# Dealing the raw groups' normalizations and products into the first three groups of a graph layer's loop

## The chip, the core and the metric

The kernel runs on one core of a Trainium2 chip. A core has five engines with a queue each: PE (TensorE, matmuls; its weight loads are listed as PEld), DVE (VectorE), ACT (ScalarE), POOL (GpSimd) and SP (SyncE, which here only issues DMAs). The metric is the device time of one execution in microseconds. The profile shows one execution of it, with every instruction's start and length; "clock" is the share of full TensorE speed that the throttle granted.

## The reference

`x` holds 12500 nodes of 128 values; 200000 edges lead from `src` to `dst`, sorted by `dst`, each of one of four types.

```python
h = jnp.maximum(_layernorm(x, axis=-1), 0.0)
xs = h[src]
for i in range(4):
    mask = (edge_type_4 == i)[:, None]
    msgs = msgs + jnp.where(mask, xs @ W[i] + b[i], 0.0)
out = x + segment_sum(msgs, dst, num_segments=N)
```

Edges are worked on in chunks of 128. The draw of `dst` puts many edges on the first nodes and few on the last.

## The kernel before, in words

**Three kinds of chunks.** The first `C0` = 528 chunks go to about 1480 much-used nodes. They are not gathered: for each of these nodes the kernel counts how often each source node and type occurs (a *slot* is one chunk's share of a node) and multiplies the counts with the whole table of normalized rows. The chunks behind them are taken in groups of `G` = 16. Groups 0 to 2 (`RAW` = 3) are the *raw* groups: their rows of `x` are gathered before the table exists, and are normalized by themselves. Groups 3 and up are the loop's: their rows are gathered from the finished table `htab`.

**The prologue.** It normalizes all nodes and writes `htab` in bfloat16 triples (`first_part` to `third_part`), gathers the raw rows (`gather_raw`, tile `hx`), and builds the slots (`make_slots`). Here the framework's scheduler sets the order on every engine. Then `add_up_raw` runs for the raw groups, one after the other: statistics and one-hots on DVE (`looks`, `oh`), 16 normalizations on ACT (L461), products of rows with one-hots on PE in float32 (L635), counts by type (L641), the weight product (L648) into the bank `raw_py`, and copies by ACT between them. All 48 columns sets are copied once to an `xo` buffer (L1283).

**The loop** (from `ordered` on) keeps the program's own order on PE, DVE and ACT. Each group has eight parts of two chunks. In a part PE multiplies the pair's rows with their one-hots (L578); a stretch of `dense_work`, the counting, follows; then DVE gets its share of the side work: one-hots of the next group (L561), adds of the group before into the ring of sums (`ring_adds`, L666), flushes of finished stretches of the ring (L691 to L713), which are decided by `goes`. The group before is weighed in the first and third part (L596, L603, L605). DVE makes a slot's two one-hots (L957 and L965, or L961), PE counts a unit of two or three slots with L983, ACT copies it (L989). The slots' one-hots are made in sets of four, about two sets ahead of PE. Units are counted in batches: 20 units first, then 27 each. When a batch is counted, `multiply` streams the table through four buffers `hs` (L1029, 576 KB each, issued by SP) and multiplies (L1033, three a node block), beside the counting of the next batch. `pace` says how far the counting must be after each part: equal numbers of PE columns for each group from `LEAD` = 3 to the last full one, where a group's own columns count too.

**Queues.** POOL issues the loop's gathers (L544), one DMA a chunk, 16 a group, one group ahead, into 11 buffers for two chunks each. The gathers of the first groups are held by `gates`: before, nine normalizations of the raw rows (`ties`) and ten marks of slot-making. SP issues the table's writes, the `hs` loads, the next blocks' indices (L210) and the loads and stores of results.

Of the kernel before, what the change touches and what calls it, by code (L numbers as in the profile page):

```python
# [35 lines left out]
F32 = mybir.dt.float32  # L36
# [31 lines left out]
LEAD = RAW  # L68
SOON = (RAW * 16) + HG
# [5 lines left out]
def kernel(  # L75
# [171 lines left out]
    rawp = early.enter_context(tc.tile_pool(name="raws", bufs=RAW * G // HG))  # L247
# [139 lines left out]
    iota_f = prep.tile([P, KR], F32, name="iota_f", bufs=1)  # L387
    nc.vector.tensor_copy(iota_f, iota_i[:, :KR])
# [29 lines left out]
    pick_f = prep.tile([P, NT, N3], F32, name="pick_f", bufs=1)  # L418
    nc.vector.tensor_copy(pick_f, pick)

# [11 lines left out]
    def look(xt, n, tag, wide):  # L432

        sums2 = aheads.tile([P, wide, 2], F32, name="mv" + tag)
        var = aheads.tile([P, wide], F32, name="var" + tag)
        rstd = aheads.tile([P, wide], F32, name="rstd" + tag)
        nmr = aheads.tile([P, wide], F32, name="nmr" + tag)
        st = aheads.tile([P, wide, 2, 3], F32, name="st" + tag)
# [171 lines left out]
    def add_up_raw(t0, g, rows, marked):  # L610
        win = window_of(C0 + t0)
        K = NT * win
        row = lambda k: rows(k)
        looks, spread, root, scales, normalize = look(row, g, "r", G)
# [4 lines left out]
        oh = rawp.tile([P, G, KR], F32, name="ohf", bufs=2)[:, :, :K]  # L619
# [8 lines left out]
        done = [normalize(k, row(k)) for k in range(g)]  # L628
        marked.extend(done[4::5])
        yield True  # L630
        sb = spool.tile([P, G * KM], F32, name="sb")[:, : G * K].rearrange("p (g t n) -> p g t n", g=G, t=NT)
        for i0 in range(0, g, SG):
            ps = s_ps.tile([P, 512], F32, name="ps")[:, : SG * K].rearrange("p (i n) -> p i n", i=SG)
            for i in range(i0, i0 + SG):
                nc.tensor.matmul(ps[:, i - i0, :], rows(i), oh[:, i, :], start=True, stop=True)  # L635
# [3 lines left out]
        pc = s_ps.tile([P, 512], F32, name="ps")[:N3, : G * win].rearrange("p (g n) -> p g n", g=G)  # L639
        for t in range(NT):  # L640
            nc.tensor.matmul(pc, pick_f[:, t, :], ohv[:, :, t, :], start=(t == 0), stop=(t == NT - 1))  # L641
        cnt = spool.tile([N3, G * WIN], BF16, name="cnt")[:, : G * win].rearrange("p (g n) -> p g n", g=G)
# [623 lines left out]
    for g in groups:  # L1266
        for _ in g:
            pass
# [35 lines left out]
    for gi, (t0, g) in list(enumerate(zip(starts, sizes)))[RAW:]:  # L1304
# [17 lines left out]
        for j, part in enumerate(sum_up(t0, g, *now, gi >= FULL)):  # L1322
# [5 lines left out]
            for f in late:  # L1328
                f()
# [192 lines left out]
```

## Time and profile before

| | |
|---|---|
| runs | 1647.18 us median of 3 (1646.1 to 1649.81) |
| profiled execution | 1651.06 us, span 1649.2 us |
| busy share of the span | PE 88%, DVE 63%, POOL 61%, ACT 28% |
| mean granted clock | 0.957 |
| moved by DMA | 317.02 MB, 192 GB/s |

Groups of instructions are named by line, engine, operation and tiles. A row of the busy time by stage gives the stretch, its length, then for each engine busy microseconds with the number of instructions, then the clock, the share of DMA time and the DMA rate. Rows of the timeline and of the chain of waits begin with start and length in microseconds. Matmuls overlap, so the starts of neighbouring rows tell the rate of PE, and their lengths do not.

### The profile page before, as it was taken

The numbers are of one execution on the slowest core, as the hardware profiler recorded it, in microseconds if no ns is written. First come the engines' busy times: TensorE is split into PE (matmuls) and PEld (weight loads), VectorE is DVE, ScalarE is ACT, GpSimd is POOL, SyncE is SP. The second block draws the span as 40 slices with busy tenths as digits, with TensorE's granted clock in tenths as the row PEclk, the third lists the DMA queues.
The fourth block names the chain that finished last, engine by engine and source line by source line (L and its number), as shares of the span: only waits on it lengthen the run. The fifth ranks groups of instructions, "written<-read, shape, count | busy, mean of one in ns | idle before, by whom it ended". The sixth has DMA issues, their size and how long they took to land.

```text
span 1649.2 us, 33169 instructions
## 1 busy us (share of the span) xinstructions
PE 1457.4 (88%) x11293; PEld 958.5 (58%) x11293; DVE 1041.5 (63%) x5387; ACT 458.7 (28%) x1121; POOL 1011.6 (61%) x1062
## 2 busy tenths in 40 slices
PE   5678789999899999999999999999999999998975
PEld 2236476666566566666666666656565656565654
DVE  8792977666585766657576666657564756574333
ACT  6494222222222222222222222222222222222011
POOL 7435566666666666666666666666666566666562
PEclk9785799999999999999999999999999999999997
DMA  7452377766667766666666667666666566666652
GB/s 221 129 212 75 107 220 220 217 197 213 200 206 211 217 194 212 197 208 208 207 202 201 200 209 220 181 210 203 180 219 198 175 194 211 184 189 193 210 169 70
DMA packets 138411, 317.02 MB, mean 192 GB/s; under 512 B 25880, under 2 KB 78666, under 8 KB 138235
## 3 DMA queue, kind: packets, MB, share of 16 engines
q1 hardware_dynamic: 89323, 214.61, 41.7%
q0 software_dynamic: 48912, 100.24, 20.8%
q8 instruction: 89, 1.46, 0.4%
q14 instruction: 87, 0.71, 0.1%
HBM read 298.71 MB, written 16.04 MB: 191 GB/s over the span
## 4 chain that ended last, share of the span: by engine, by line
PE 81%; issue 8%; DVE 8%; ACT 2%; DMA 1%; DVEq 0%; SPq 0%; POOL 0%; ACTq 0%
PE pa L1033 47%; PE pt L983 12%; PE py L605 7%; PE ps L578 7%; DVE o L957 1%; PE pt L1047 1%; PE ps L635 1%; PE py L596 1%; PE pt L691 1%; DVE oh L561 1%; DVE o L965 1%; DVE ring L666 1%; PE pt L857 1%; DVE stt L440 1%; PE pt L854 0%
## 5 line engine op out<-in xcount | busy, mean ns | idle before, releaser
L544 POOL DMA_INDIRECT hm<-htab,srcT x987 | 954.7, 967 | 575.6 <-issue 226.0
L1033 PE MATMUL pa<-counts,hs 128*128 128x324 fp8e4 (+1 forms) x5586 | 1000.5, 304 | 50.2 <-issue 47.1
L1033 PEld LDWEIGHTS <-hs 128*128 128x128 bf16 x5586 | 519.0, 96 | 325.1 <-issue 84.7
L957 DVE TENSOR_SCALAR o<-iota_n,hkT 128x392 bf16<-128x392 f16 x1211 | 401.2, 331 | 75.4 <-PE pt L983 30.6
L983 PE MATMUL pt<-o,o 128*128 128x396 bf16 x1211 | 378.4, 336 | 37.0 <-DVE o L965 20.0
L989 ACT CAST counts<-pt 128x396 int32<-128x396 f32 x506 | 242.1, 493 | 500.5 <-PE pt L983 172.1
L561 DVE TENSOR_SCALAR oh<-iota_b,keyT 128x56 bf16<-128x56 bf16 (+8 forms) x987 | 167.7, 261 | 265.6 <-PE ps L578 94.6
L581 ACT COPY sb<-ps 128x224 f32<-128x224 f32 (+8 forms) x247 | 98.4, 399 | 480.3 <-PE pt L983 165.0
L578 PE MATMUL ps<-oh,hm 128*128 128x56 bf16 (+8 forms) x2961 | 189.1, 198 | 38.0 <-issue 35.3
L578 PEld LDWEIGHTS <-hm 128*128 128x128 bf16 x2961 | 163.0, 99 | 96.5 <-issue 49.1
L666 DVE TENSOR_TENSOR ring<-ring,py 128x14 f32 (+7 forms) x960 | 167.7, 175 | 65.0 <-PE pa L1033 13.0
L965 DVE TENSOR_SCALAR o<-iota,loT 128x128 bf16<-128x128 bf16 x660 | 178.4, 270 | 0.0
L983 PEld LDWEIGHTS <-o 128*128 128x128 bf16 x1211 | 114.8, 97 | 96.2 <-DVE o L965 27.4
L965 DVE TENSOR_SCALAR o<-iota,loT,byT 128x128 bf16<-128x128 bf16 x461 | 155.4, 337 | 0.0
L605 PE MATMUL py<-sb,wsb 128*128 128x224 f32 (+7 forms) x480 | 129.5, 412 | 1.3 <-issue 1.0
L605 PEld LDWEIGHTS py<-sb,wsb 128*128 128x128 f32 x480 | 88.2, 196 | 27.6 <-issue 5.6
L997 DVE COPY bi<-counts 128x27 int32<-128x27 int32 (+1 forms) x19 | 4.2, 220 | 113.3 <-issue 64.7
L528 POOL DMA_INDIRECT hx<-in_x_dram,srcT x48 | 51.3, 1069 | 35.9 <-DVE stt L440 22.4
L600 ACT CAST cnt<-py 128x224 bf16<-128x224 f32 (+7 forms) x60 | 23.7, 396 | 93.3 <-PE ps L578 29.9
L461 ACT ACTIVATE h<-hm,nmrt,rstdt 128x128 f32<-128x128 f32 x98 | 43.0, 493 | 1.0 <-DVE mvt L444 0.5
L1047 PE MATMUL pt<-sd,wsb 128*128 128x81 f32 (+1 forms) x152 | 25.8, 325 | 4.6 <-issue 4.6
L490 PE MATMUL ps<-h,ident 128*128 128x384 f32 (+1 forms) x34 | 16.3, 563 | 12.7 <-issue 11.6
(235 smaller groups left out, 666.6 us busy)
## 6 DMA issues: line engine op xcount, KB each, us to landing
hs<-htab SPq DMA_DIRECT2D x304, 576.0 KB
hm<-htab,srcT POOLq DMA_INDIRECT x987
htab<-h SPq DMA_DIRECT2D x32, 288.0 KB
xo<-in_x_dram SPq DMA_DIRECT2D x24, 256.0 KB
out_dram<-xo SPq DMA_DIRECT2D x24, 256.0 KB
hs<-htab SPq DMA_DIRECT2D x19, 192.0 KB
hm<-in_x_dram SPq DMA_DIRECT2D x18, 192.0 KB
hm<-in_x_dram SPq DMA_DIRECT2D x14, 168.0 KB
```

The lines of the kernel that those rows point to most:

```text
L528: one = nc.gpsimd.indirect_dma_start(out=hm[:, i * D : (i + 1) * D], out_offset=None, in_=x, in_offset=bass.IndirectOffsetOnAxis(ap=srcf[: ...
L544: one = nc.gpsimd.indirect_dma_start(out=hm[:, (i - h0) * D3 : (i - h0 + 1) * D3], out_offset=None, in_=htab, in_offset=bass.IndirectOffse ...
L561: nc.vector.tensor_scalar(oh[:, i, :], iota_b[:, :K], keyf[:, at : at + 1], None, ALU.is_equal)
L578: nc.tensor.matmul(ps[:, i - i0, :], rows(i, c), oh[:, i, :], start=(c == 0), stop=(c == 2))
L581: nc.scalar.copy(sb[:, i0:i1].rearrange("p g t n -> p g (t n)"), ps[:, : i1 - i0, :])
L605: nc.tensor.matmul(py[:, :g, :], wsb[:, t, :], sb[:, :g, t, :], start=False, stop=(t == NT - 1))
L666: nc.vector.tensor_tensor(to, to, of(i), ALU.add)
L957: one = nc.vector.tensor_scalar(o2[:, k, :NB], iota_n, hkT[:, s : s + 1], None, ALU.is_equal)
L965: one = nc.vector.tensor_scalar(o1[:, k], iota_1, loT[:, s : s + 1], by, ALU.is_equal, ALU.mult)
L983: one = nc.tensor.matmul(pb, o1, o2, start=first, stop=last)
L989: nc.scalar.copy(counts[:, :, i * NT : (i + 1) * NT], pb.rearrange("p (b t) -> p b t", t=NT))
L1033: nc.tensor.matmul(pa[:, : 3 * nu * NT].rearrange("p (m v) -> p m v", m=3), hs[:, j - j0, c * D : (c + 1) * D], of, start=(j == 0 and c == 0),
```

## The change

The raw groups' products and most of their normalizations are dealt into the loop. Before the loop only the statistics, the one-hots and the scales of the three groups and the first four normalizations of group 0 are left. `raw_work` goes through 18 steps (six for each raw group: four of four products each with the next four normalizations, one of type counts, one of the weight product), spread over the 24 parts of loop groups 3, 4 and 5. The products take their PSUM banks from `x_ps` (four, shared with the counting) instead of `s_ps`, and have their own `sbr` and `cntr` tiles.

`pace` adds `RAW_COLUMNS` = 1920 columns for each chunk to each of these three groups, so that less counting falls into them and more into each later group. The pool of raw rows stays open until the end of group 5, on the right side of memory; therefore the second buffer of counts (`dense2`) and the four `hs` buffers come only then. The copy of the raw sums follows group 5, all 48 raw ring adds are dealt in group 6, and the earliest group with a flush is 4 instead of 3. The gates of the first gathers are 19 marks of slot-making.

```diff
+RAW_COLUMNS = 1920
...
-    rawp = early.enter_context(tc.tile_pool(name="raws", bufs=RAW * G // HG))
...
+        for k in range(SG):
+            normalize(k, rows(k))
+        yield True
+        sb = rawp.tile([P, G * KR], F32, name="sbr", bufs=1)[:, : G * K].rearrange("p (g t n) -> p g t n", g=G, t=NT)
         for i0 in range(0, g, SG):
-            ps = s_ps.tile([P, 512], F32, name="ps")[:, : SG * K].rearrange("p (i n) -> p i n", i=SG)
+            ps = x_ps.tile([P, 512], F32, name="pt")[:, : SG * K].rearrange("p (i n) -> p i n", i=SG)
             for i in range(i0, i0 + SG):
                 nc.tensor.matmul(ps[:, i - i0, :], rows(i), oh[:, i, :], start=True, stop=True)
+            for k in range(i0 + SG, min(i0 + 2 * SG, g)):
+                normalize(k, rows(k))
             nc.scalar.copy(sb[:, i0 : i0 + SG].rearrange("p g t n -> p g (t n)"), ps)
             yield True
...
-        next((i for i in [*range(RAW, FULL), final - 1] if starts[i] + sizes[i] >= c), final)
+        next((i for i in [*range(RAW + 1, FULL), final - 1] if starts[i] + sizes[i] >= c), final)
...
-        own = [columns(i) for i in range(LEAD, last)]
+        own = [columns(i) + (G * RAW_COLUMNS if i < LEAD + RAW else 0) for i in range(LEAD, last)]
...
-                now = vs, dense.tile([P, NW + 1, UB * NT], I32, name="counts")
+                now = vs, dense[batches.index(vs) % 2].tile([P, NW + 1, UB * NT], I32, name="counts")
...
     for g in groups:
-        for _ in g:
-            pass
+        next(g)
+        next(g)
+    next(groups[0])
+
+    def raw_work():
+        for m, g in enumerate(groups):
+            for n, _ in enumerate(g):
+                if n == G // SG - 1 and m + 1 < RAW:
+                    next(groups[m + 1])
+                yield True
...
-    gates.extend(ties + marks[len(marks) - (20 - 1 - len(ties)) :])
+    gates.extend(marks[-19:])
+    raw_steps = raw_work()
+    raw_done = 0
+    raw_all = RAW * (G // SG + 2)
...
+        if gi == 2 * RAW:
+            side += raw_adds
...
+            while gi < 2 * RAW and raw_done < raw_all and raw_done * RAW * parts < ((gi - RAW) * parts + j + 1) * raw_all:
+                next(raw_steps)
+                raw_done += 1
...
+        if gi == 2 * RAW - 1:
...
+            nc.scalar.copy(raw_sums, raw_py[:, : RAW * G * win_raw])
...
+            raw_stack.close()
+            dense.append(counting.enter_context(tc.tile_pool(name="dense2", bufs=1)))
+            hsp = counting.enter_context(tc.tile_pool(name="hsp", bufs=STREAM))
```

More of the change, by code (lines that the diff above doesn't have):

```diff
@@ L607, in weigh, with add_up_raw @@
         yield True
[L610 removed]
+    def add_up_raw(t0, g, rows):
         win = window_of(C0 + t0)
         K = NT * win
[L613 to L614 removed]
+        looks, spread, root, scales, normalize = look(rows, g, "r", G, rawp, RAW)
         for l in looks:
```

55 lines of the change are left out of this document (25 added, 30 removed).

## The prediction

> **What bounds the kernel now.** I read the page's busy shares and slices first, then the busy time by stage, the chain of waits around 118 to 154 us, the timelines of POOL and DVE there, and the first L596 matmul of each group as the border between groups (the row of 232.40 below is group 5's, issued behind the first pair of group 6).
>
> ```profile
> span 1649.2 us, 33169 instructions
> PE 1457.4 (88%) x11293; PEld 958.5 (58%) x11293; DVE 1041.5 (63%) x5387; ACT 458.7 (28%) x1121; POOL 1011.6 (61%) x1062
> ...
> PE   5678789999899999999999999999999999998975
> ...
> PEclk9785799999999999999999999999999999999997
> ...
> L1033 PE MATMUL pa<-counts,hs 128*128 128x324 fp8e4 (+1 forms) x5586 | 1000.5, 304 | 50.2 <-issue 47.1
> ...
> L666 DVE TENSOR_TENSOR ring<-ring,py 128x14 f32 (+7 forms) x960 | 167.7, 175 | 65.0 <-PE pa L1033 13.0
> ```
> ```profile
> 232.40 0.26 PE L596 MATMUL py<-oh,three 128*32 128x192 bf16 x3
> ```
> ```profile
> core 0: us, PE busy (x) PEld busy (x) DVE busy (x) ACT busy (x) POOL busy (x), PEclk, DMA share, GB/s
> 117.34:154.18 36.84, 33.17 (x141) 28.42 (x142) 10.26 (x55) 22.32 (x63) 21.01 (x22) 0.50 0.37 120
> 154.18:180.50 26.32, 13.10 (x98) 6.01 (x98) 20.84 (x107) 8.77 (x22) 17.15 (x18) 0.69 0.32 87
> 180.50:206.36 25.86, 22.31 (x186) 16.00 (x185) 24.22 (x136) 7.29 (x19) 13.74 (x15) 0.77 0.44 128
> 206.36:232.40 26.04, 23.27 (x218) 18.61 (x217) 21.41 (x93) 7.34 (x18) 16.79 (x16) 0.93 0.73 229
> 232.40:257.23 24.83, 22.67 (x213) 17.26 (x212) 17.08 (x94) 5.47 (x14) 15.27 (x16) 1.00 0.70 221
> 257.23:279.98 22.75, 21.30 (x184) 14.40 (x183) 16.05 (x82) 6.01 (x16) 14.52 (x16) 1.00 0.70 215
> 232.40:1596.88 1364.48, 1255.82 (x10139) 832.91 (x10139) 843.17 (x4443) 325.53 (x778) 866.59 (x897) 0.99 0.66 202
> ```
>
> The first row is the raw stage: groups 0 to 2 alone, PE busy 33 of 37 us at half clock. The next three are loop groups 3, 4 and 5, paced by DVE (24.22 of 25.86 us busy in group 4), which makes the one-hots of slots. From 232.40 on PE sets the pace: 92% busy at a clock of 0.99, 57 groups in 1364.48 us, 23.9 us each.
>
> So two things can be saved, the 37 us in which nothing but raw work runs and the slack of three DVE-paced groups, and there is one place where they are paid back: each matmul that leaves groups 3 to 5 comes again in the PE-bound part.
>
> **The change part by part.** *What is moved.* The instruction order of both programs gives the work between the L596 borders. Before, groups 3, 4 and 5 hold 97 slot-counting matmuls (L983, 128x396) and 216 multiplying ones (L1033, 128x240). Changed, they hold 31 and none, and beside them the raw work: 48 rows, 12 pick matmuls and 12 of L648's kind. Thus 66 and 216 matmuls are deferred. Group 6 then holds 36 and 72 (before 23 and 99), group 7 28 and 135 (before 23 and 102). The 48 raw ring adds move from groups 3 and 4 into group 6.
>
> *When the loop can reach group 6.* The gathers of the loop's rows are issued one by one on POOL:
>
> ```profile
> 117.34 0.94 POOL L544 DMA_INDIRECT hm<-htab,srcT  x1 [21.56 <-ACT rstdr L452]
> 118.59 0.95 POOL L544 DMA_INDIRECT hm<-htab,srcT  x1 [0.30 <-issue]
> ...
> 127.56 0.95 POOL L544 DMA_INDIRECT hm<-htab,srcT  x1 [0.30 <-issue]
> 132.14 0.94 POOL L544 DMA_INDIRECT hm<-htab,srcT  x1 [3.64 <-ACT hx L461]
> ```
> ```profile
> 279.37 0.94 POOL hm L544
> ...
> 280.62 2.97 DMA hm<-htab,srcT
> ```
>
> They start when the table is written, at 117.34, and step by 1.25 us. Before, they were held by normalizations (3.64 us at 132.14), harmlessly, for PE was busy with raw work. The changed gates are marks of slot-making, which is over when the table ends, so only the table holds the first gather. On SP the first index load of the next block now stands among the last table writes, for +0.3 us, and the four loads of hs no longer follow them:
>
> ```profile
> 115.72 1.90 SPq L1029 DMA_DIRECT2D hs<-htab  x4
> 154.18 0.33 SPq L210 DMA_DIRECT2D si<-in_src_dram  x1
> ```
>
> A group needs 16 gathers, 20 us. The second gather of group 6 is number 50: 117.6 + 49 x 1.25 = 178.9; a gather lands 4.2 us after its start (279.37 to 283.59), so 183.1. With that pair's matmuls and counting, the border that stood at 232.40 comes at 184.5 if nothing is slower than POOL.
>
> Is anything slower? PE, at the raw stage's half clock:
>
> ```profile
> 135.19 4.97 PE ps L635 x24
> 140.17 2.24 PE ps L641 x8
> ...
> 144.08 2.43 PE pa L648 x8
> ```
> ```profile
> 188.66 2.21 PE py L605 x8
> 190.88 0.20 PE ps L578 x6
> ...
> 193.37 0.64 PE pa L1033 x6
> 194.00 0.17 PE pt L983
> ...
> 273.23 0.43 PE pa L1033 x3
> ```
>
> Raw: 96 halves x 0.207 = 19.9 us, picks 3 x 2.24, products 3 x (2.43 + 0.24). Own: 144 of L578 at 0.04 = 5.8, two L605 sets 5.3. Counting 31 at 0.34 (twice the full-clock 0.17) = 10.5. Sum 56 us against 60 us of gathers; PE can start at about 124, when DVE has made the first set, which ends at 180 without a wait. So PE is just under POOL. DVE has some 10 to 13 us a group to do, ACT 16 normalizations a group (6.27 us by the row below) plus copies, some 12 us. I take 184.5; below, 182.5 (a landing of 2.2 us); above, 26 us a group, as these groups took before, 202.
>
> ```profile
> 117.50 6.27 ACT L461 ACTIVATE hx<-hx,nmrr,rstdr 128x128 f32<-128x128 f32 x16 [0.35 <-DVE nmrr L456]
> ```
>
> *Group 6.* DVE now has the ring adds of all three raw groups:
>
> ```profile
> 163.91 0.78 DVE L666 TENSOR_TENSOR ring<-ring,xo 128x10 f32 x4 [1.15 <-issue]
> 164.62 0.32 DVE L957 TENSOR_SCALAR o<-iota_n,hkT 128x392 bf16<-128x392 f16 x1
> ...
> 168.22 0.77 DVE L666 TENSOR_TENSOR ring<-ring,xo 128x10 f32 x4
> ...
> 210.03 1.60 DVE L561 TENSOR_SCALAR oh<-iota_b,keyT 128x48 bf16<-128x48 bf16 x9
> ...
> 214.95 1.75 DVE L708 TENSOR_TENSOR acc<-acc,ring 128x1536 f32<-128x1536 f32 x1
> 217.09 1.34 DVE L713 MEMSET ring<- 128x1536 f32 x1 [0.39 <-DVE acc L708]
> ```
>
> By the order, PE's last counting of group 6 needs 34 slots (eight took 164.62 to 168.22: 0.45 each, 15.3), 48 raw adds (four in 0.71: 8.6), 13 row one-hots (0.17: 2.2), three register loads (by L666's row 65.0 us idle over 960/16 = 60 sets: 1.1 each, 3.3), sums 0.8 and the copy of the raw sums 0.8. That is 31 us against 24.83 before: +6.2 (bounds 24.8, as before, and 36, with each load at twice its price and the slots at 0.5). PE's own work there is 18 us at full clock, so DVE decides; if PE fell to half clock there, 31 too. Behind the adds on DVE stand the slots that PE waits for, and SP's next load into a sums buffer (xo) with the fifth load of hs behind it; the four first hs loads cover exactly the 72 multiplications of group 6, so this costs nothing unless the adds last past the group. Those four loads (formerly prefetched at 115.72) now wait for the last raw product and have some 10 us of counting to land behind.
>
> *Group 7* has the first flush (1.75 + 1.34), now a group later, and 28 slots, 24 adds, 19 one-hots, two loads: 26 us of DVE, 26.5 taken, against 22.75: +3.7.
>
> *The deferred matmuls.* At the end of group 7 the changed kernel is behind by 48 slots (143 less 95) x 0.167 = 8.0 us, 87 narrow multiplications x 0.107 = 9.3 and 123 wide ones x 0.143 = 17.6: 34.9 us of PE at full clock, dealt over 55 groups. The loop's PE is 92% busy, and what idles there is mostly issue; I take 37, between 26 (a quarter fills idle time) and 38 (34.9 / 0.92).
>
> *The sum against the profiled span:* 184.5 - 232.4 = -47.9; +6.2; +3.7; +37: -1.0 us, 1648 us of span. The profiled execution took 1651.06 (span 1649.2 and 1.9 around it), 3.9 above the median 1647.18 of the runs shown; the same difference gives 1646. Copies of iota_f and pick_f, pool places and the PSUM buffers of x_ps instead of s_ps I cost at nothing: the two copies (each no larger than a ring add's kind) replace two that the program made before, and the PSUM buffers are freed by ACT copies, from a queue with some 12 us of work in 20; without that cover each of groups 3 to 5 would lose the 1 to 2 us that are in the slower rival.
>
> [...] The clock during the raw stage:
>
> ```profile
> 132.00:136.00 4.00, 4.00 (x18) 3.78 (x17) 0.00 (x0) 4.00 (x11) 2.94 (x4) 0.50 0.18 49
> 148.00:152.00 4.00, 4.00 (x20) 3.88 (x20) 0.00 (x0) 0.58 (x2) 3.08 (x4) 0.50 0.31 85
> ```
>
> PE was busy all of both stretches and still had half clock: the short float32 products do not raise it here, so I count groups 3 to 5 at half clock. [...]
>
> **The rivals.** *PE, not POOL, paces groups 3 to 5 (slower).* The 56 us of half-clock work fill 93% of the gather time, in a fixed order in which each raw product waits for ACT, each slot for DVE and each pair for its gather. If waits add 3 us a group, 23 us a group, the border comes at about 193: +8.5, so 1655. Groups 5 and 6 before took 26.04 and 24.83 although no engine was busy beyond 23.27, which speaks for it; against it, that each raw step has a step's time between its parts. It decides against the change from 21.5 us a group on (border 188.8). Chance 0.36.
>
> *The deferred matmuls are cheaper (faster).* PE idles 108.7 us between 232.40 and 1596.88. If a quarter of the deferred matmuls falls into stretches in which PE would have waited for DVE or a gather, 37 becomes 26, -11: 1636. For it, that 108.7 us are there; against it, that at L1033 47.1 of 50.2 idle us are issue, which comes with each instruction wherever it stands. A clock that rises in group 6 doesn't help, DVE bounds it. Chance 0.26.
>
> *Paid back as summed (no change).* Chance 0.38. That the counting isn't thinned is excluded by the order: 31 against 97.
>
> **How the numbers follow.** A measurement of this kernel can tell about 0.2%, 3.3 us. The likeliest single case is no change, 1646, its own range 1643 to 1650. The range takes in the faster rival short of its end (1638: border at 182.5, deferred at 30) and the slower one past its price (1658: border at 196). Faster 0.26, same 0.38, slower 0.36.
>
> **What would show it.** After: gathers 1.25 us apart from 117.5 to about 178 with hardly a wait for PE; the border of group 6 at 183 to 187; PE clock about 0.5 to 0.7 till then; group 6 near 31 us with DVE full; group 7 near 26; later groups 0.6 to 0.7 us longer than before. The prediction is wrong if gathers wait for PE before 178, if group 6 takes 24 or 36 us, or if later groups grow by less than 0.4 us or more than 0.9.

## The result, and the profile after

The changed kernel took 1658.88 us (median of 4 runs, 1655.3 to 1660.82) beside 1646.64 us of the kernel before (1646.04 to 1649.81): a ratio of 1.0061, 95% interval [1.0045, 1.0077], slower by 0.6%. Forecast were 1646 us and no change.

Busy time by stage of the changed kernel (the columns are those of the first row). The stages are: up to the first gather of the loop, groups 3, 4 and 5 up to the border of group 6 (the L591 matmul, L596 before), group 6, group 7, the later groups, the end.

```profile
core 0: us, PE busy (x) PEld busy (x) DVE busy (x) ACT busy (x) POOL busy (x), PEclk, DMA share, GB/s
0.00:118.84 118.84, 78.14 (x288) 32.74 (x288) 99.93 (x448) 80.38 (x205) 54.36 (x76) 0.91 0.55 175
118.84:169.30 50.46, 19.11 (x122) 15.18 (x122) 17.27 (x86) 11.51 (x32) 34.66 (x36) 0.51 0.27 71
169.30:192.83 23.53, 16.61 (x121) 13.92 (x120) 8.57 (x48) 10.64 (x32) 15.17 (x16) 0.71 0.26 71
192.83:215.27 22.44, 18.12 (x115) 12.96 (x114) 10.18 (x56) 9.23 (x27) 14.73 (x16) 0.64 0.28 69
215.27:252.62 37.35, 21.47 (x171) 15.22 (x171) 30.26 (x155) 9.42 (x23) 21.72 (x21) 0.82 0.58 198
252.62:276.59 23.97, 23.97 (x224) 19.20 (x223) 19.06 (x98) 7.76 (x18) 13.63 (x14) 0.91 0.64 190
276.59:1602.09 1325.50, 1247.60 (x10029) 828.60 (x10029) 826.35 (x4381) 322.20 (x768) 841.04 (x865) 0.99 0.67 205
1602.09:1653.60 51.51, 29.68 (x230) 22.32 (x229) 22.71 (x117) 7.34 (x17) 19.75 (x21) 0.77 0.36 102
```

The same view of the kernel before, for the later groups:

```profile
279.98:1596.88 1316.90, 1211.86 (x9745) 801.24 (x9745) 810.04 (x4268) 314.05 (x749) 836.80 (x867) 0.99 0.66 201
```

Against the rows shown in the prediction (span 1649.2 before, 1653.6 after):

| | before | after | difference | forecast |
|---|---|---|---|---|
| up to the border of group 6 | 232.40 | 215.27 | -17.1 | -47.9 |
| group 6 | 24.83 | 37.35 | +12.5 | +6.2 |
| group 7 | 22.75 | 23.97 | +1.2 | +3.7 |
| later groups and end | 1369.2 | 1377.0 | +7.8 | +37 |
| span | 1649.2 | 1653.6 | +4.4 | -1.0 |

Two terms are far off and in opposite directions: the way to group 6 saved 31 us less than summed, and the deferred matmuls cost 29 us less. The medians differ by 12.2 us and the two spans by 4.4: the profiled execution of before lies 4.4 us above its median, that of after 3.6 below. In which stage those 7.8 us lie, one profile of each can't tell.

Most of the 31 us lie in group 3, which took 50.46 us from the first gather on where about 25 were summed, with PE busy for 19.11 of them. The timeline of PE in it (start, length, then the instruction, in brackets the idle time before it and what ended it):

```profile
151.29 0.23 PE L630 MATMUL pt<-ohf,hx 128*128 128x40 f32 x1 [1.88 <-issue]
153.39 0.23 PE L630 MATMUL pt<-ohf,hx 128*128 128x40 f32 x1 [1.87 <-issue]
155.49 0.22 PE L630 MATMUL pt<-ohf,hx 128*128 128x40 f32 x1 [1.87 <-issue]
155.52 0.39 PE L573 MATMUL ps<-oh,hm 128*128 128x40 bf16 x6
```

and of POOL in the same stretch:

```profile
150.71 0.94 POOL L539 DMA_INDIRECT hm<-htab,srcT  x1 [0.30 <-issue]
155.74 0.94 POOL L539 DMA_INDIRECT hm<-htab,srcT  x1 [4.09 <-PE pt L630]
```

PE starts single matmuls 2.10 us apart, with no wait that the trace knows: "issue". At 155.49 this ends, and six matmuls start at once. The last gather before had ended at 151.65. The next one then waited 4.09 us for PE, so from there on the gathers were late too. DVE shows the same between 133.7 and 142.2 us: about one instruction per 0.70 us or a multiple of it, in step with PE. Then it stands:

```profile
157.15 0.32 DVE L954 TENSOR_SCALAR o<-iota_n,hkT 128x392 bf16<-128x392 f16 x1 [14.72 <-PE ps L573]
```

ACT waits for PE, 9.94 us up to 142.91 and 10.97 us up to 155.71. Between the two it makes four normalizations in 1.65 us, as long as it took for four ahead of the stretch; the expectations below that count ACT among the slowed engines are wrong in this. In this kernel 1,759 of PE's instructions change a semaphore that the other engines wait for; I call such a change a release. The trace has a release of PE at 142.88, none from there to 155.48 us, and then six within 0.21 us. I call such a stretch a hold-up.

Group 6, in the groups of DVE's instructions between 215.27 and 252.62 us (count, busy us, mean ns, idle us just before them and what ended it):

```profile
L954 DVE TENSOR_SCALAR o<-iota_n,hkT 128x392 bf16<-128x392 f16 x33 | 10.5, 317 | 0.0
L663 DVE TENSOR_TENSOR ring<-ring,xo 128x10 f32 x48 | 8.1, 170 | 8.4 <-ACT xo L1364 4.4 <-issue 2.3 <-DVE ring L663 0.3
...
L663 DVE TENSOR_TENSOR ring<-ring,py 128x12 f32 x16 | 2.7, 166 | 0.5
...
L705 DVE TENSOR_TENSOR acc<-acc,ring 128x1536 f32<-128x1536 f32 x1 | 1.8, 1752 | 0.0
L710 DVE MEMSET ring<- 128x1536 f32 x1 | 1.3, 1338 | 0.4 <-DVE acc L705 0.4
```

DVE was busy for 30.26 of the group's 37.35 us, so it does set its length: 33 slots with their second one-hots, the 48 raw adds with the waits before them, but also the group's own 16 adds and the first flush.

And the page's group of the multiplications, whose row before had 50.2 us of idle time, 47.1 of it issue:

```profile
L1030 PE MATMUL pa<-counts,hs 128*128 128x324 fp8e4 (+1 forms) x5586 | 999.9, 304 | 28.5 <-issue 24.6
```

With more matmuls behind group 7, the "issue" time at this line halved.

### The profile page after: what moved, and what is told of

It is laid out like the page before. It is cut to its first block, busy times and chain, and to the rows that moved or that the text cites. A ratio compares the mean times of both kernels' runs of the same rounds, so it can differ in the third digit from the quotient of the medians.

```text
span 1653.6 us, 33161 instructions
## 1 busy us (share of the span) xinstructions
PE 1454.7 (88%) x11293; PEld 960.1 (58%) x11293; DVE 1034.3 (63%) x5387; ACT 458.5 (28%) x1121; POOL 1015.1 (61%) x1062
## 2 busy tenths in 40 slices
DMA packets 138411, 317.02 MB, mean 192 GB/s; under 512 B 25880, under 2 KB 78666, under 8 KB 138235
## 4 chain that ended last, share of the span: by engine, by line
PE 78%; DVE 9%; issue 7%; another core or an unknown queue 2%; ACT 2%; DMA 1%; DVEq 1%; SPq 0%; POOL 0%; ACTq 0%; POOLq 0%
PE pa L1030 45%; PE pt L980 12%; PE py L600 7%; PE ps L573 6%; DVE o L954 2%; DVE ring L663 1%; PE pt L1044 1%; PE py L591 1%; DVE o L962 1%; PE pt L630 1%; DVE oh L556 1%; PE pt L854 1%; PE pt L688 1%; DVE stt L435 1%
## 5 line engine op out<-in xcount | busy, mean ns | idle before, releaser
L1030 PE MATMUL pa<-counts,hs 128*128 128x324 fp8e4 (+1 forms) x5586 | 999.9, 304 | 28.5 <-issue 24.6
L954 DVE TENSOR_SCALAR o<-iota_n,hkT 128x392 bf16<-128x392 f16 x1211 | 395.6, 327 | 87.9 <-PE ps L573 32.1
L980 PE MATMUL pt<-o,o 128*128 128x396 bf16 x1211 | 385.4, 340 | 33.5 <-DVE o L962 14.9
L630 PE MATMUL pt<-ohf,hx 128*128 128x40 f32 x96 | 20.3, 360 | 21.4 <-issue 12.8
L630 PEld LDWEIGHTS pt<-ohf,hx 128*128 128x128 f32 x96 | 19.9, 283 | 24.7 <-issue 12.8
```

Source lines behind the costliest of these rows:

```text
L954: one = nc.vector.tensor_scalar(o2[:, k, :NB], iota_n, hkT[:, s : s + 1], None, ALU.is_equal)
L980: one = nc.tensor.matmul(pb, o1, o2, start=first, stop=last)
L1030: nc.tensor.matmul(pa[:, : 3 * nu * NT].rearrange("p (m v) -> p m v", m=3), hs[:, j - j0, c * D : (c + 1) * D], of, start=(j == 0 and c == 0),
```

## Experiments

### The same two programs on other chips

Edit: none. The changed kernel again, and later both kernels together.

> The changed kernel once more, for a second trace of it. In its first trace group 3 took 47 us (122 to 169) in place of the 20 that the forecast gave it, and from 131 to 165 us PE, DVE and ACT often began one instruction each 0.70 us or a multiple of it, with no wait that the trace shows. Theory 'it belongs to the kernel': the stretch comes again between 125 and 170 us, and the first matmul of group 4's end (L591) stands again near 169 us. Rival 'a pause from outside that hit this one execution': group 3 takes 20 to 30 us here, the border behind it stands at 142 to 152 us, and the pause, if any, stands elsewhere.

> The kernel before, unchanged, for a second trace of it. The last four kernels ran on another chip than those ahead of them: the kernel before took 1468.4 us there and 1650.0 on the first, and there no trace shows instructions held up beside long runs of gathers (up to 162 in a row). If this run is on the faster chip again: groups 7 on take 22 us each, PE idles little behind the border of group 6 (some 12 us in 1250), and what the dealt kernels lose there (1495 to 1502 against 1468) is read from this trace. If on a chip like the first: 1649 to 1654 us, groups 3 to 5 at 26 us each.

> The changed kernel, unchanged, beside it. On a chip without hold-ups: groups 3 to 5 take 20 to 22 us each, as forecast (the border of group 6 near 180 us), group 6 takes 36 to 38 as in the kernel with fills (36.4), and the deferred matmuls cost what PE needs for them, 35 to 40 us, as forecast: 2 to 3.5% slower than before (1497 to 1520 us). Rival: the fills cost the 2%, and the changed kernel without them is within 0.7% of before there too. On a chip with hold-ups: group 3 takes 47 to 50 us, 0.2 to 0.8% slower than before.

On the chip of the first of these, before took 1650.01 us (27 runs) and after 1655.45: 1.0028 [1.0014, 1.0043], span 1657.6. The first gather stood at 120.34, the border of group 4 at 170.6, group 6 took 40.3 us. So the late border and the long group 6 came again. The later groups and the end took 1376.5 us there (1377.0 in the result), and 1367.1 in the kernel before with only the flush moved, on the same chip: the small growth behind group 7 comes again too. The loss is smaller than on the chip of the result, and the intervals just don't touch.

The chip of the other two ran the same program before in 1468.77 us, 11% faster. The unchanged copy gave 0.9999 [0.9989, 1.0008], the changed kernel 1495.81 us: 1.0188 [1.0170, 1.0205]. Busy time by stage there, before (columns as above):

```profile
0.00:100.24 100.24, 72.53 (x288) 31.17 (x288) 97.42 (x442) 79.79 (x204) 56.71 (x75) 0.98 0.65 206
100.24:162.80 62.56, 46.52 (x240) 34.59 (x240) 31.16 (x162) 31.40 (x85) 38.55 (x40) 0.58 0.36 108
162.80:188.90 26.10, 22.36 (x186) 16.05 (x186) 24.43 (x134) 8.46 (x21) 15.09 (x17) 0.76 0.51 145
188.90:210.40 21.50, 21.02 (x219) 17.44 (x218) 20.43 (x91) 7.99 (x19) 16.36 (x16) 1.00 0.88 278
210.40:232.30 21.90, 21.90 (x215) 17.13 (x214) 17.96 (x98) 5.30 (x13) 16.54 (x18) 1.00 0.80 253
232.30:253.20 20.90, 20.90 (x184) 14.21 (x183) 15.32 (x83) 6.79 (x16) 15.22 (x17) 1.00 0.77 224
253.20:1423.70 1170.50, 1166.06 (x9745) 795.51 (x9744) 805.27 (x4268) 327.78 (x747) 838.57 (x863) 1.00 0.74 226
```

and after:

```profile
0.00:104.45 104.45, 71.97 (x288) 31.38 (x288) 98.86 (x446) 79.47 (x204) 54.10 (x76) 0.97 0.63 199
104.45:130.50 26.05, 17.41 (x126) 13.85 (x126) 16.01 (x88) 12.56 (x36) 19.96 (x21) 0.60 0.29 78
130.50:151.30 20.80, 16.87 (x121) 13.67 (x120) 8.74 (x48) 11.57 (x35) 15.87 (x17) 0.70 0.32 85
151.30:170.27 18.97, 15.62 (x115) 12.12 (x114) 11.83 (x63) 8.61 (x25) 14.33 (x15) 0.70 0.34 85
170.27:206.87 36.60, 20.36 (x170) 14.50 (x170) 29.92 (x149) 8.50 (x21) 28.20 (x28) 0.82 0.64 214
206.87:230.50 23.63, 23.63 (x224) 19.05 (x223) 19.33 (x98) 8.43 (x19) 18.15 (x19) 0.92 0.75 229
230.50:1451.50 1221.00, 1208.68 (x10032) 824.83 (x10031) 831.15 (x4381) 337.52 (x767) 843.95 (x870) 1.00 0.73 223
```

The runs behind the result met five chips, of these two sorts and none between. I call them A (before took 1646.64 in the result, 1650.01 in the runs e1 to e4, 1648.60 in e13 and e14) and B (1468.42 in e5 to e8, 1468.77 in e9 to e12, 1469.07 and 1467.65 in e15 to e18). Before is 183.8 us of span shorter on B: 17.1 ahead of the first gather, 9.7 in the raw stage and groups 3 to 7, 146.4 in the later groups, 10.6 at the end. Over the 987 gathers of the loop every kernel stepped 1.524 to 1.539 us a gather on A (before 1.529, after 1.533), and 1.368 (before) to 1.405 on B. There are no hold-ups on B, although up to 228 gathers ran there in a row (thinning alone, below), and at the multiplications all of PE's idle time in before is 0.5 us there, a wait for ACT and not "issue".

Another difference runs through every trace, that of before too. ACT's copy of the products of rows with one-hots (L581 in before) can start when the last of their matmuls (L578) has ended. From the nearest end of such a matmul ahead of it, it started a median 0.04 us later in each of the 12 traces on B, and a median 0.85 to 1.27 us later in the 8 traces on A (1.21 in before, 0.85 in after). Counted from the end of its own last matmul, and only where ACT had ended its work before by then, it is 1.50 us in before (81 copies) and 1.66 in after (99), in the two traces of the result. The kernel before, first on A, then on B:

```profile
604.66 0.32 PE L578 MATMUL ps<-oh,hm 128*128 128x56 bf16 x6
606.48 0.34 ACT L581 COPY sb<-ps 128x224 f32<-128x224 f32 x1 [2.50 <-PE pt L983]
```

```profile
303.85 0.31 PE L578 MATMUL ps<-oh,hm 128*128 128x48 bf16 x6
304.19 0.32 ACT L581 COPY sb<-ps 128x192 f32<-128x192 f32 x1 [1.93 <-PE ps L578]
```

So on A releases of PE reach ACT late by this measure in the whole loop, and not only in hold-ups. Why is open.

On B the forecast's terms can be read without hold-ups. From the first gather to the border of group 6, 110.2 us became 65.8 (-44.3). Ahead of the first gather 4.2 us were lost: the table's last write is issued at 101.3 instead of 97.4. That the scheduler orders the changed prologue otherwise is the likely reason, and not tested. Group 6 +14.7, group 7 +2.7, later groups +50.5, end +0.3: +28.1 together. All stages summed, PE was busy 1399.1 us before and 1402.3 after: it is PE's idle time that grew, from 66.3 to 91.2.

The groups of PE's instructions in the later groups on B, before and after:

```profile
L1033 PE MATMUL pa<-counts,hs 128*128 128x324 fp8e4 x5155 | 914.7, 305 | 0.5 <-ACT sd L1043 0.5
L983 PE MATMUL pt<-o,o 128*128 128x396 bf16 x1066 | 329.6, 329 | 3.6 <-DVE o L965 3.6
```

```profile
L1030 PE MATMUL pa<-counts,hs 128*128 128x324 fp8e4 (+1 forms) x5380 | 951.7, 304 | 0.5 <-ACT sd L1040 0.5
L980 PE MATMUL pt<-o,o 128*128 128x396 bf16 x1116 | 346.5, 330 | 11.5 <-DVE o L962 11.4
```

There are 283 more matmuls behind group 7: 225 multiplications, 50 countings and 8 that close a node block. 225 x 0.145 + 50 x 0.167 + 8 x 0.17 = 42.3 us (each price is the mean or median time from one matmul's start to the next), and PE was busy 42.6 us longer (1208.68 less 1166.06). The other 7.9 us are idle time: PE waited 11.4 us for one-hots of DVE at the counting where it had waited 3.6.

### The hold-ups of group 3

First theory: products at half clock are slow by themselves. Second: a long unbroken run of gathers holds the other engines up. Third: a rate of gathers that is too high over some time does it. The runs: thinning in the kernel before, without dealing; six row buffers, so that gathers stop earlier; a fill of 0.75 us on POOL ahead of every fourth gather of groups 3 to 5; and a POOL copy that makes each pair of gathers wait for the pair before.

```diff
+RAW_COLUMNS = 1920
-        own = [columns(i) for i in range(LEAD, last)]
+        own = [columns(i) + (G * RAW_COLUMNS if i < LEAD + RAW else 0) for i in range(LEAD, last)]
```

> The kernel before, with nothing but the added 1,920 columns a slice in the planner: counting is thinner in groups 3 to 5 with nothing in the place of it, products and normalizations stay ahead of the loop. It prices the deferral by itself. Forecast's price (37 us for the deferred matmuls, later groups 0.6 to 0.7 us longer): groups 3 to 5 take 20 us each in place of 26 (border of group 6 near 214 in place of 232), and the span is 1649 - 18 + 37 = 1668 us. Rival 'deferred matmuls fall into time in which PE idles anyway' (8 us in the changed kernel's trace): 1649 - 18 + 8 = 1639 us. Third: groups 3 to 5 do not get shorter, because the gathers or DVE pace them: 1649 to 1660 us.

```diff
-    hpool = mid.enter_context(tc.tile_pool(name="rows", bufs=11))
+    hpool = mid.enter_context(tc.tile_pool(name="rows", bufs=6))
```

> The changed kernel with 6 buffers of gathered rows in place of 11, so that at most 12 gathers can run ahead of PE (22 before). In three traces of the dealt kernels POOL issued 26 to 28 gathers back to back from 119 us on, and from the 13th or so PE, DVE and ACT began about one instruction each 0.70 us until 3 to 4 us after the run of gathers ended; in the kernel with thinner counting alone a run of 20 (203.6 to 230.7) had PE's signals come 12 us late, all at once at 233.2. Theory 'a long unbroken run of gathers holds up the other engines': the run from 119 us ends after 12 to 16 gathers, group 3 takes 24 to 32 us in place of 47 to 50, the border behind it stands at 143 to 152 us. Rival 'the raw products and normalizations in the loop are slow by themselves': 45 to 50 us stay. Later groups may lose where 11 buffers were needed.

```diff
             hm = hpool.tile([P, HG * D3], BF16, name="hm")
+            if t0 < 2 * RAW * G and h0 // HG % 2 == 0:
+                nc.gpsimd.memset(hm, 0.0)
```

> The changed kernel with 11 buffers, and one small fill of the buffer to come (128 x 768, on POOL) ahead of every fourth gather of groups 3 to 5: more work for POOL and as many gathers ahead, but no run of more than 4 gathers. Theory 'an unbroken run of gathers holds up the others': group 3 takes 22 to 30 us (16 gathers of 1.25 us and 4 fills of about 1 us), the border behind it stands near 143 to 150 us, the one-instruction-per-0.70-us stretch is gone, and the end comes 10 to 20 us earlier (1634 to 1644 us of span). Rival 'what counts is how many gathers are ahead, not the unbroken run': 45 to 50 us stay. Rival 'the products are slow by themselves': 45 us or more stay. Rival 'given back later': group 3 is short, the end moves by less than 4 us.

> The changed kernel with a fill on POOL ahead of every fourth gather of groups 3 to 5. On a chip without hold-ups: as the changed kernel within 5 us, since group 3 has no stop to lose there. On a chip with hold-ups, theory 'an unbroken run of gathers holds up the others': group 3 takes 22 to 30 us in place of 47; rival 'the number of gathers ahead, or the products': 45 us or more.

> The changed kernel with a fill on POOL ahead of every fourth gather of groups 3 to 5, hoped for on a chip with hold-ups, where it hasn't run. Theory 'an unbroken run of gathers holds up the others': group 3 takes 22 to 30 us there in place of 47, and no stretch of one instruction each 0.70 us stands between 130 and 160 us. Rival 'the gathers ahead of PE, broken or not' or 'the products': 45 us or more. On a chip without hold-ups it is a repeat: 1500 us, 2.2% over before.

```diff
+            if t0 < 2 * RAW * G and paced:
+                nc.gpsimd.tensor_copy(hm[:, :8], paced[-1][:, HG * D3 - 8 :])
+            paced.append(hm)
```

> The changed kernel with the gathers of groups 3 to 5 held to pairs: a copy of 8 columns on POOL that reads the pair before and writes the pair to come makes each pair wait until the one before has landed, some 1.9 us a gather in place of 1.25. On the chips with hold-ups every kernel so far steps 1.52 to 1.54 us a gather over all its 987, on the others 1.37 to 1.39, and the breaks of 0.9 us after every fourth gather (1.48 us a gather) only put the hold-ups off from the 13th to the 40th gather. Theory 'what counts is the rate of the gathers; more than one each 1.5 to 1.6 us builds up a backlog that holds the others up': on such a chip no instruction of PE, DVE or ACT stands 0.7 us apart in groups 3 to 5, and they take 27 to 31 us each, the border of group 6 at 118 + 48 x 1.9 = 205 to 215 us, as early as with gathers at full speed (215 to 222). Rival 'the raw products in the loop are held up by themselves': group 3 keeps 40 us or more, the border at 225 us or later. On a chip without hold-ups: groups 3 to 5 some 30 us each, 25 us later in all than the changed kernel there.

> The changed kernel with the gathers of groups 3 to 5 held to pairs, once more, hoped for on a chip with hold-ups (its first run met one without). There, theory 'the rate of the gathers counts': no instruction of PE, DVE or ACT stands 0.7 us apart in groups 3 to 5, which take 27 to 32 us each; the border of group 6 comes at 205 to 217 us, as early as with gathers at full speed (215 to 222). Rival 'the raw products in the loop are held up by themselves': group 3 keeps 40 us or more, the border at 225 us or later.

*Thinning alone, on A* (e3): 1651.93 us, 1.0014 [1.0003, 1.0026]. Here the raw work stands ahead of the loop as before, and a hold-up comes later, in group 6 (37.9 us instead of 24.8). PE there, and POOL beside it:

```profile
219.93 1.07 PE L984 MATMUL pt<-o,o 128*128 128x396 bf16 x5
236.33 1.50 PE L984 MATMUL pt<-o,o 128*128 128x396 bf16 x4 [15.33 <-DVE o L966]
```

```profile
229.74 0.95 POOL L545 DMA_INDIRECT hm<-htab,srcT  x1 [0.30 <-issue]
233.45 0.94 POOL L545 DMA_INDIRECT hm<-htab,srcT  x1 [2.76 <-remote]
```

PE stood from 221 to 236 us beside gathers that ran without a break from 203.6 to 230.7. The trace puts PE's wait down to a DVE one-hot, DVE's own wait (13.37 us up to 234.35) down to a copy of counts by ACT, and ACT's to a release that it doesn't name:

```profile
233.21 0.32 ACT L582 COPY sb<-ps 128x192 f32<-128x192 f32 x1 [12.24 <-remote]
```

PE's matmuls had ended by 221.0, but none of PE's releases reach the others from 220.5 to 233.2 us, and then six do at once; ACT and the gather at 233.45 started right behind them. So hold-ups don't need the raw products. On B the products don't slow group 3 either: it takes 26.05 us from the first gather on. The first theory falls. Against before, this kernel won 20.0 us up to the border of group 6, lost 13.1 in it and 9.7 in all that follows, so the deferral alone is as cheap on A as in the result.

*Fills.* Three times the kernel with fills: on B 1501.78 us, 1.0229 [1.0212, 1.0246], and 1501.51, 1.0222 [1.0205, 1.0239], with groups 4 and 5 at about 21 us each and nothing to cure (some 6 us more than after). On A 1659.52, 1.0057 [1.0036, 1.0079]. PE's timeline on A:

```profile
153.00 0.32 PE L593 MATMUL py<-oh,three 128*32 128x160 bf16 x4
...
182.75 0.19 PE L575 MATMUL ps<-oh,hm 128*128 128x40 bf16 x1 [1.00 <-issue]
184.86 0.19 PE L575 MATMUL ps<-oh,hm 128*128 128x40 bf16 x1 [1.92 <-issue]
```

Group 3 now took some 31 us from the first gather (121.8) to its end, but steps of 0.7 us or a multiple come between 170 and 200 instead (2.1 us from 182.75 to 184.86), and group 4 takes 40.8 us. POOL had made 36 gathers by 172, at 1.42 us each, fills included; in the changed kernel and its repetition the hold-up began after some 13 gathers at 1.25 us. So no unbroken run is needed, and the second theory falls in this form. The third agrees with both: if a gather could be digested in 1.53 us only, the rate of the whole loop on A, 13 gathers would be 3.6 us behind (0.28 each) and 36 some 3.9 (0.11 each), and in group 3 the hold-up ended 3.8 us after the last gather. That is an estimate that fits, and nothing more; and it fits only if the hold-up is counted from 170, for a first wait of 7.1 us for a late release stands on PE at 156.8 already, after 25 gathers.

*Six buffers and paired gathers* were meant to test that, and ran on B only. Six buffers: 1517.95, 1.0342 [1.0325, 1.0359]. Against the changed kernel on B the first gather stood 11.6 us later and the end took 9.8 us more, for reasons that no run shows; from the first gather to the border of group 6 it took 65.3 us (65.8). Paired gathers: 1497.96, 1.0197 [1.0180, 1.0214], and 1500.93, 1.0221 [1.0196, 1.0247]. The pairs came out at 1.31 us a gather, where 1.9 were expected, and there was no hold-up that they could have removed. Both are undecided.

### The parts alone: thinning and the later flush

Edits: the thinning above, on a chip B too; the same with fills up to group 8 (`t0 < 3 * RAW * G`); and in the kernel before

```diff
-        next((i for i in [*range(RAW, FULL), final - 1] if starts[i] + sizes[i] >= c), final)
+        next((i for i in [*range(RAW + 1, FULL), final - 1] if starts[i] + sizes[i] >= c), final)
```

> The kernel before with thinner counting in groups 3 to 5 and nothing else. It prices the deferral by itself. On a chip without hold-ups: groups 3 to 5 take 16 to 20 us each (fewer matmuls there, 10 to 18 us won), the deferred matmuls cost 35 to 40 us, and the sum is 15 to 30 us over before. Rival 'deferral is free, group 6 alone loses': within 8 us of before. On a chip with hold-ups: 2 us over before, as in the first run of it.

> The kernel before with thinner counting alone (products and normalizations ahead of the loop), and the fills in groups 3 to 8. In its trace without them group 6 took 38.0 us with a stop from 221 to 233 us beside a run of 20 gathers. Theory 'unbroken run': no stop, group 6 takes 23 to 28 us, groups 3 to 5 some 20 to 24 each, span 1652 less 8 to 12 = 1640 to 1644 us. Rival 'group 6 waits for counts or the first loads of hs': it keeps 35 us or more, span 1650 to 1654.

> The kernel before, with the first flush a group later and nothing else. Theory 'costs nothing': 1646 us within 2 us, groups 4 to 6 within 1 us of before. Rival: its loads of xo, moved, meet the first loads of hs on SP and delay group 5 or 6 by 3 us or more.

Thinning alone on B: 1489.72 us, 1.0139 [1.0123, 1.0156]. By stage, groups 3 to 5 with the raw stage ahead of them, and the later groups:

```profile
100.97:181.10 80.13, 53.57 (x356) 43.01 (x357) 44.90 (x239) 33.29 (x95) 54.34 (x55) 0.63 0.36 106
...
225.00:1446.20 1221.20, 1208.17 (x10028) 824.41 (x10027) 833.95 (x4381) 337.40 (x767) 852.02 (x879) 1.00 0.73 224
```

Against before on B, 110.2 us became 80.1 (-30.0), group 6 didn't change, group 7 +1.1, and the later groups +50.7. So the thinning loses 22.8 us of span by itself, and what is dealt and moved beside it only 5.3 more: -14.3 in groups 3 to 5, and +14.7 in group 6, +3.5 ahead of the first gather, +1.6 in group 7. With fills on B 1502.92, 1.0238 [1.0221, 1.0255]: fills cost 13 us there and have nothing to cure.

The later flush alone, on A: 1652.73, 1.0012 [1.0000, 1.0024]. It moved 3.1 us of DVE work into group 6, which took 30.8 us instead of 24.83; later groups gave that back, and the span was 1649.2. What it costs is within what can be told.

On A, of the 47.1 us of "issue" time that before has at the multiplications, 47.0 are left with the later flush alone, and 27.2 with thinning alone (e3). So it is the deferred matmuls that fill it.

### The adds of group 6

Edit: the sums of each raw group are copied as soon as it is done, and 32 of the 48 raw adds run in groups 4 and 5.

```diff
+                if n == G // SG + 1 and m + 1 < RAW:
+                    part = rawp.tile([P, G * win_raw], F32, name="rsum", bufs=1)
+                    nc.scalar.copy(part, raw_py[:, m * G * win_raw : (m + 1) * G * win_raw])
+                    adds.extend(
+                        ring_adds(m * G, G, lambda i, part=part: part[:, i * win_raw : (i + 1) * win_raw], win_raw)
+                    )
...
-            for m in range(RAW):
+            for m in range(RAW - 1, RAW):
```

> The changed kernel, with 32 of the 48 ring adds of the raw groups taken out of group 6: the sums of the first two raw groups are copied out of PSUM when each is done, and added in groups 4 and 5, where DVE has room; the last 16 stay in group 6. Theory 'DVE bounds group 6' (DVE 30.26 busy of its 37.35 us, 48 adds at 0.196 us = 9.4): 32 adds fewer are 6.3 us, so group 6 takes 30 to 32 us, and the end comes 4 to 7 us earlier. Rival 'the counts and the first loads of hs set group 6': it keeps 35 to 38 us. Second rival 'the later groups take it back': group 6 is shorter, and the end moves by less than 2 us.

With the fills as well:

> The fills of the run before together with the early ring adds (32 of 48 adds in groups 4 and 5). If both reasons hold and add up: group 3 at 22 to 30 us, group 6 at 28 to 32, span 1654.3 - 15 to 20 = 1634 to 1640 us, which would be under the kernel before. If the later groups give it back: 1648 to 1654 us.

On A 1653.32, 1.0024 [1.0009, 1.0040]. The borders of group 6 and of group 7 in PE's timeline:

```profile
220.60 0.35 PE L591 MATMUL py<-oh,three 128*32 128x192 bf16 x4
...
250.88 0.35 PE L591 MATMUL py<-oh,three 128*32 128x192 bf16 x4 [1.91 <-DVE ring L663]
```

Group 6 took 30.3 us instead of 40.3 in the unchanged repetition on the same chip. Groups 4 and 5, which hold the adds now, took 4.9 and 3.9 us more than there, the border of group 7 came 5.5 us earlier and the end 3.3 (4 to 7 were expected). On B with fills group 6 took 31.0 instead of 36.4, and 1495.15 us stand beside 1501.78: 6.6 us gained. So DVE sets group 6, and adds that have room in groups 4 and 5 are cheaper there. The loss of the whole change stays.

### Less thinning

Edit: `RAW_COLUMNS` 1500 instead of 1920, which leaves 51 slots in groups 3 to 5 (31 in the changed kernel, 97 before). Alone, and with the early adds of the section before:

```diff
-RAW_COLUMNS = 1920
+RAW_COLUMNS = 1500
```

> The changed kernel with 1,500 columns in place of 1,920 and nothing else (51 slots counted in groups 3 to 5 in place of 31), to part the two edits that together took the cost on chips without hold-ups from 1.9% to 0.2%. On such a chip: if the early adds are worth 6 us (as group 6 showed) and the rest is the thinner thinning, 0.6 to 0.8% over before; rival 'the adds in group 6 push the loss on', 1.2% or more. On a chip with hold-ups: 0.1 to 0.5% over before.

> The changed kernel with 32 of the 48 raw ring adds in groups 4 and 5, and 1,500 columns in place of 1,920 in the planner: 51 slots are counted in groups 3 to 5 in place of 31 (97 before), and at the end of group 7 it is behind the kernel before by 39 slots and 147 multiplications in place of 48 and 210. Theory 'the loss is matmuls moved out of time in which PE idles beside the gathers, and DVE in group 6': on a chip without hold-ups group 6 takes 28 to 31 us, the later groups cost 50.4 x 186/258 = 36 us in place of 50, groups 3 to 5 at most 4 us more, so 0.6 to 1.1% over before in place of 1.9%. Rival 'the later groups pay for something else, not for the number deferred': 1.5% or more. On a chip with hold-ups: within 0.3% of before.

> The kernel of the earlier run with 1,500 columns and early ring adds, hoped for on a chip without hold-ups. There: group 6 at 27 to 31 us, the later groups 30 to 40 us over before in place of 50, in all 0.6 to 1.2% over before (the changed kernel 1.9%). Rival: 1.5% or more, if the later groups pay for something else than the number of matmuls deferred. On a chip with hold-ups: again within 0.3% of before.

Alone, on B: 1481.42, 1.0083 [1.0064, 1.0102], against 1.0188 with 1920. With the early adds on B 1471.31, 1.0020 [1.0011, 1.0030], and on A 1649.40, 1.0006 [0.9989, 1.0023]. By stage on B, the last kernel's groups 3 to 5 and later groups:

```profile
105.90:179.00 73.10, 52.05 (x376) 38.51 (x376) 48.37 (x260) 36.22 (x103) 55.74 (x58) 0.69 0.40 115
...
225.30:1429.70 1204.40, 1196.83 (x9956) 816.20 (x9955) 829.81 (x4378) 335.09 (x762) 852.19 (x874) 1.00 0.74 225
```

The last is better than expected: beside the 1500 columns the early adds were worth 10 us on B and not 6, 8.1 of them in group 6 (24.5 instead of 32.6 us).

Groups 3 to 5 saved 37.0 us (73.1 instead of 110.2), the later groups paid 34.0 for 211 more matmuls; 283 had cost 50.5. So the later price goes with the matmuls, about 0.15 us each and some idle time, and the first 20 slots that come back into groups 3 to 5 cost them only 7 us. How little thinning the dealing allows was not measured: the second buffer of counts is opened only when the raw rows' pool is closed, behind group 5. On neither sort of chip does any of these kernels beat the one before.

## Why the prediction was wrong, point by point

**"184.5 if nothing is slower than POOL."** This step failed on the chip of the result: the border came at 215.27. The first gather stood at 118.84 (117.6 forecast), and of the 30.8 us most is the hold-up in group 3, which no row that the prediction shows tells of. There, the first run was nine gathers long and then broken; the normalization that broke it (3.64 us at 132.14) was called harmless, since PE had raw work. On chips B the step holds: 65.8 us from the first gather to the border, and 184.5 less 117.6 is 66.9. PE's clock, priced at half in the prediction, was 0.51, 0.71 and 0.64 in the three groups on A and 0.60, 0.70 and 0.70 on B. PE was busy 53.8 us there on A and 49.9 on B, not 56, and it bounded neither. The landing of a gather was misread as well, by 1 to 2 us: the row shown, 280.62 and 2.97 us long, belongs to the second of two gathers, and by their packets gathers are done 2.3 us after their start, near the 2.2 of the lower bound.

**Group 6, 31 us.** DVE does decide, with 30.26 of 37.35 us busy on A and 29.92 of 36.60 on B. Two terms were left out: the group's own 16 adds (2.7 + 0.5 us idle) and the first flush (1.8 + 1.3 + 0.4), which the sum had put into group 7. 31 + 3.2 + 3.5 = 37.7. What was named stood as summed: the 48 adds took 8.1 us (8.6), and the idle time before them, 5.4 us inside the group (8.4 less 3.0 ahead of the border), is near the 4.9 put for loads and copies. It is an error of bookkeeping in both places; group 7 came in lower (23.97, 26.5 forecast) by about the flush.

**The deferred matmuls, 37 us.** The count was wrong first: 283 matmuls and not 258, since group 6 before was taken as 99 multiplications where its order holds 117, and 87 were priced as narrow (0.107) where a multiplication behind group 7 takes 0.145 in the mean. On B, where PE is busy in all but 4.4 of 1170.5 us, this shows: 42.6 us of busy time, and 7.9 of waiting for DVE that the sum had at nothing. On A the same matmuls cost 35.7 us of PE time (1247.60 less 1211.86), but the later groups and the end grew by 7.8 only, for PE's idle time there fell from 105.0 to 77.9. The failed sentence is "47.1 of 50.2 idle us are issue, which comes with each instruction wherever it stands". It does not: at the same line it is 24.6 us in the changed kernel, 27.2 with thinning alone, and nothing on B. On A more PE work fills it, so I take it for time in which something other than PE sets the pace. That this is the gathers' rate is argued from 1.53 us a gather in every kernel on A, and not shown. PE's late releases on A are a second candidate, and no run parts the two.

**The rivals.** The slower one gave 1655 and named PE's waits in groups 3 to 5; the place and the sign are right, but it was one stop of some 22 us in group 3 and not 3 us in each group. The faster one (part of the deferred matmuls falls into idle time) is what happened on A, with far more than its quarter. Either alone would have been a large error: as the two large errors have opposite signs, it is luck that the forecast came out only 12.9 us low, the median 0.9 above the range. "No change" would have been the wrong forecast on B by 28 us, for reasons that lie in the count and in group 6, and not in any hold-up: -40.1 to the border of group 6, +14.7, +2.7 and +50.8.

**What would show it right or wrong**, as listed there: the gathers waited for PE well before 178, group 6 took more than 36 us, and the later groups grew by 0.14 us each on A (7.8 over 55) and by 0.92 on B. All three marks fell outside.

## What to carry to other kernels

Moving matmuls out of a stage in which PE has slack into one in which it is full has a price per matmul, to be counted from the order of the instructions in both programs (here, on B, 0.15 us for each of 283); it must be set against how much shorter the first stage really becomes, and a half-way step (51 slots and not 31, with the ring adds moved as well) nearly broke even. Where moved work lands on an engine, list everything that this engine does there, its regular share and what the same edit shifts as well, before the sum is made. Idle time called "issue" on the engine that should be the bound hid added work here: on A 47.1 us of it stood at the multiplications before and 24.6 after. Run the same program on a second chip before taking such idle time for the kernel's own.

## What the runs showed of the hardware

The same program took 1468 us on some chips and 1648 on others, 11% apart, each chip steady within 0.6%, and a change that cost 0.3 to 0.6% on the one sort cost 1.9% on the other. On the slower sort ACT's copy starts a median 0.85 to 1.27 us after the nearest end of the matmuls ahead of it, on the faster one 0.04 us. Beside dense gathers on POOL (1.25 us apart, 1.42 with fills) there are hold-ups of 15 to 30 us on the slower sort: PE, and in group 3 DVE too, fall into steps of 0.70 us or a multiple, or PE stands, and no release of PE is recorded for long (12.6 and 12.7 us in the two shown above). The gathers' own data keep coming all the while (first packet 1.66 us and done 2.3 us after the start of the instruction, on both sorts). What differs in the chips stays open. The traces differ in one more thing: those of the slower sort hold about a third as many records of semaphore changes (9,892 to 10,335 in a trace, against 29,259 to 29,571), with as many instructions (33,169 in before and 33,161 in after, on both sorts) and DMA packets (138,411). Of PE's 1,759 releases in the changed kernel 1,644 are recorded on A. No run here shows whether the hold-ups and the missing records have one cause, nor whether an execution that is not recorded has hold-ups. Open stays also which rate or amount of gathers starts a hold-up: the two kernels meant for that met chips without any.
